# A depthwise 7x7 convolution recast: from 128-row banded filter weights to 28-row image weights in four quarters of the PE array

## The chip, the cores and the metric

The kernel runs on one core of one Trainium2 chip. The metric is device time in microseconds (us) of the whole program, from one launch. A core has five engines that run their own instruction streams: TensorE (PE in the profile, with its weight loads shown apart as PEld), VectorE (DVE), ScalarE (ACT), GpSimd (POOL) and SyncE (SP), which here only issues DMAs. All data are fp32.

## The reference

The input x is (32, 384, 28, 28): 32 images of 384 channels, 784 pixels each. Two layers follow each other. Cut to what matters:

```python
# layer 0: a ConvNeXt block
y = depthwise_conv7x7(x, dw_w, padding=3) + dw_b        # 384 channels, each with its own 7x7 filter
y = layernorm_over_channels(y) * ln_g + ln_b            # mean and variance over 384 channels per pixel
y = gelu(y @ w1 + b1)                                   # 384 -> 1536
gx = sqrt(sum_over_pixels(y * y)); nx = gx / (mean(gx) + eps)
y = grn_g * (y * nx) + grn_b + y
x = x + (y @ w2 + b2)                                   # 1536 -> 384
# layer 1: a gate
avg, mx, mn = mean, max, min of x over pixels           # per image and channel
logits = concat(avg @ W1.T, grouped(mx), mn @ W3.T) @ Wfc.T
out = sigmoid(logits[:, :, None, None] + x)
```

## The kernel before

**Two stages.** The first stage does the depthwise convolution of all 32 images and stores its result `yd` in device memory. It also prepares weights: the two matrices w1 and w2 are multiplied with fast (Strassen-like) schemes, so linear combinations of their blocks are formed once by GpSimd and ScalarE (`form_w`, stored to `u1d` and `u2d`), after w1 was centred for the layer norm (`center_w`). The second stage loops over images: `up` (products with `u1d`, PE line 979), gelu and norm, `down` (products with `u2d`, PE line 1139), `gate_store`. It starts with `finish`, which turns the sums over channels into the reciprocal standard deviation `rsd`. Its PE work is ordered image after image.

**The convolution on PE, before.** Partitions hold 4 image rows of 32 padded pixels (`PW` = 32). For each channel a banded 128x(128+2*96) matrix, `tmat`, holds the 7x7 filter in every position; it is loaded by one DMA for 8 channels from `fs`, a table of filter sequences in device memory, with an access pattern that shifts by one element per partition. `tmat` is the stationary operand (the weights), the turned image `xt` is the moving one. Per channel `conv` issues three products: the middle block (line 718, 224 moving columns, 7 row groups x 32 images), the rows that follow (line 720, 192 columns) and the rows before (line 722, 192 columns). Two channels share one PSUM tile `pc`.

**What feeds it and what follows it.** `load_x` brings a group of 4 images and 32 channels; `pad_x` copies it to a padded tile (ScalarE, line 506; at first also GpSimd); `turn_x` has PE transpose it, 7 pieces of 128x128 (line 516), and VectorE or ScalarE copy it out of PSUM into `xt` (lines 525 and 527). After the products VectorE transposes the PSUM tile in 32x32 blocks into `yt` (line 725) and adds it to `acc`, the sum over channels (line 729); ScalarE squares `yt` with the bias `dwb` added (line 735); GpSimd adds the squares to `ssum` (line 741). SP stores `yt` to `yd`. The last 16 channels are done in two halves of 16 images, so that the first image's result can be loaded back before the second half is done; `first_image` adds the bias on ScalarE while it copies image 0 to `room`.

**What sets the order.** Most instructions around the change are held in program order (`keep`); the rest (the forming of weight combinations, later the products) is placed by a list scheduler. SP's queue issues its DMAs in order. The layout of `yd` is by image row modulo 4 and reversed inside a row, so later readers use reversed, strided views (`rows`, and the quarter view in `down`).

Of the kernel before, what the change touches and what calls it, by code (L numbers as in the profile page):

```python
# [8 lines left out]
F32 = mybir.dt.float32  # L9
# [20 lines left out]
RW = 4  # L30
NJ = HW // RW
PW = P // RW
XC = 32
TC = 8
YC = 16
NB = P // XC
REACH = 3 * PW
MW = P + 2 * REACH
T0 = P - REACH

SN = 6 * PW + 7
S0 = T0 + REACH + P - 1 - 3 * PW - 3
FL = S0 + SN
YR = NJ * PW
SQ = 4
NQD = P // PW

# [166 lines left out]
def convnext_gate_kernel(  # L216
# [15 lines left out]
    N = NJ * B  # L232
# [6 lines left out]
    NY = C // YC  # L239
# [21 lines left out]
    stats = const.tile([P, SQ * YR + 2 * NJ * B], F32, name="stats")  # L261
    ssum = stats[:, : SQ * YR].rearrange("p (c n) -> p c n", n=YR)
    acc = stats[:, SQ * YR :].rearrange("p (c n) -> p c n", c=2)
# [34 lines left out]
    B0 = min(B, 16)  # L298

    def load_y(b):  # L300
        yi = yis[b] = yip.tile([P, CB, NQD, YR], F32, tag="yi", name=f"yi_{b}")

        with tc.issue_after(last_u2[-1]) if last_u2 else ExitStack():
            for cb in range(CB):
                ins = load_y_part(b, yi, cb, 0, P)
                if b == 1:
                    tc.keep_in_program_order(ins)
        load_rb(b)
# [24 lines left out]
    def rows(v):  # L333

        return v.rearrange("p q (j w) -> p (q j) w", w=PW)[:, :, ::-1][:, :, :HW]

    def normed(b, cbs=range(CB)):
# [5 lines left out]
        for cb in cbs:  # L343
            ins = nc.vector.scalar_tensor_tensor(  # L344
                accs[b][:, cb].rearrange("p (r w) -> p r w", w=HW), rows(yis[b][:, cb]),
                dwb_t[:, cb : cb + 1], rows(rbs[b]), ALU.add, ALU.mult,
# [43 lines left out]
    with ExitStack() as one:  # L390
        tp = one.enter_context(tc.tile_pool(name="tp", bufs=1))
        xtp = one.enter_context(tc.tile_pool(name="xtp", bufs=2))
        ufp = one.enter_context(tc.tile_pool(name="ufp", bufs=3))
        ycp = one.enter_context(tc.tile_pool(name="ycp", bufs=2))
        psx = one.enter_context(tc.tile_pool(name="psx", bufs=3, space=bass.MemoryType.PSUM))
        psb = one.enter_context(tc.tile_pool(name="psb", bufs=1, space=bass.MemoryType.PSUM))
        psc = one.enter_context(tc.tile_pool(name="psc", bufs=4, space=bass.MemoryType.PSUM))
        sqp = one.enter_context(tc.tile_pool(name="sqp", bufs=2))

# [18 lines left out]
        LENT = (3, 5, 7)  # L418
        AHEAD = B // NB
        NX = C // XC  # L420
        NG = B // NB
        NXI = 8
        xi_last = tp.tile([P, NT], F32, name="xi_last")
        GT = NX * NG
        xis = {}

        def load_x(i):

            k, g = divmod(i, NG)
            n = i % NXI  # L430
            t = xis[i] = xi_last if n == NXI - 1 else room[:, n * NT : (n + 1) * NT]
            base = x[g * NB, k * XC : k * XC + 1, :]
            nc.sync.dma_start(
                t,
                bass.AP(
                    tensor=base.tensor,
                    offset=base.offset,
                    ap=[[NT, XC], [C * NT, NB], [1, NT]],
                ),
            )  # L440

        dww = scratch([CB, 49])
        for i in range(AHEAD):
            load_x(i)
            if i == 1:
                nc.sync.dma_start(dww, dw_w.rearrange("(cb p) t -> p cb t", p=P))

        tab = ws[:, : CB * FL].rearrange("p (cb m) -> p cb m", m=FL)
        dwb = tp.tile([P, C], F32, name="dwb")
# [4 lines left out]
        grp_a = scratch([CB, R])  # L454


        NT2 = 4
        tmat = [tp.tile([P, TC, FL], F32, name=f"tmat_{i}") for i in range(NT2)]
        nc.vector.memset(tab, 0.0)

        def sequences(cb):
            nc.vector.tensor_copy(
                tab[:, cb, S0 : S0 + SN - 7].rearrange("p (y x) -> p y x", x=PW)[:, :, :7],
                dww[:, cb, :42].rearrange("p (y x) -> p y x", x=7),
            )
            nc.vector.tensor_copy(tab[:, cb, S0 + SN - 7 :], dww[:, cb, 42:])

        for cb in range(CB):
            sequences(cb)
            if cb == 0:  # L470
                nc.scalar.dma_start(fs[0][: 2 * TC, :], tab[: 2 * TC, 0, :])
                nc.scalar.dma_start(fs[0][2 * TC : P, :], tab[2 * TC :, 0, :])
        vrows = scratch([P], NV)
        zrow = scratch([FL], 1)
        nc.vector.memset(zrow, 0.0)
        NK = C // TC

        def load_t(s, parts=1):
            base = fs[s * TC // P]
            n = TC // parts  # L480
            for i in range(parts):
                nc.sync.dma_start(
                    tmat[s % NT2][:, i * n : (i + 1) * n, :].rearrange("p c m -> p (c m)"),
                    bass.AP(
                        tensor=base.tensor,
                        offset=base.offset + (s * TC % P + i * n) * FL,
                        ap=[[1, P], [1, n * FL]],
                    ),
                )


        NPAD = 3
# [881 lines left out]
```

## Time and profile before

| what | value |
|---|---|
| median of 3 runs | 3041.02 us (3037.3 to 3043.16) |
| the profiled execution | 3041.33 us, of which span 3039.6 us |
| PE busy over the span | 2996.2 us (99%) |
| PE's first convolution product starts | 17.69 us |
| PE's first product of `up` starts | 499.62 us |
| DMA in the first 500 us | 173.64 MB, 347 GB/s |

The span is what the profile covers; the 1.7 us around it are outside. A matmul's duration in a row is its latency; products overlap in the pipeline, so the time that one takes of PE is the step from its start to the next one's. An fp32 product appears as two weight loads and two matmuls.

### The profile page before, as it was taken

What the parts mean: (1) busy time and instruction counts of PE and PEld (TensorE: products, weight loads), DVE (VectorE), ACT (ScalarE), POOL (GpSimd) and SP (SyncE); (2) the same over time, 40 slices, a digit from 0 to 9 for tenths busy, and PEclk for the clock granted to TensorE, in tenths of its full rate; (3) what the DMA queues carried; (4) which work ended last, traced back from release to release, by engine and by line L of the source; (5) the groups of instructions that cost most, each with busy time, mean ns of one, the idle gap of its engine ahead of it and who ended that gap; (6) DMA issues with size and microseconds to landing.
All of it is one profiled execution on the core that took longest, in us unless ns stands there. A gap on an engine that the chain in (4) does not pass through costs nothing.

```text
span 3039.6 us, 43826 instructions
## 1 busy us (share of the span) xinstructions
PE 2996.2 (99%) x14436; PEld 2427.9 (80%) x14436; DVE 2036.2 (67%) x4643; ACT 1787.4 (59%) x2899; POOL 2431.9 (80%) x1811
## 2 busy tenths in 40 slices
PE   8999999899999999999999999999999999999998
PEld 8999997577777777777777777777777777777777
DVE  5767667776666666666666666666666666666665
ACT  4455554756666666666666666665666666666661
POOL 3367866688888888888888888888888888888897
PEclk9999999999999999999999999999999999999999
DMA  9899997546666666666666565566655666666645
GB/s 358 327 359 375 364 342 259 169 149 203 199 206 207 201 204 207 199 206 207 199 206 207 198 205 194 199 203 204 195 191 196 197 198 200 201 203 201 195 152 198
DMA packets 279256, 674.94 MB, mean 222 GB/s; under 512 B 24234, under 2 KB 99704, under 8 KB 273016
## 3 DMA queue, kind: packets, MB, share of 16 engines
q1 hardware_dynamic: 266472, 634.63, 61.9%
q10 hardware_dynamic: 12560, 37.51, 3.1%
q8 instruction: 117, 1.92, 0.2%
q14 instruction: 107, 0.88, 0.1%
HBM read 575.57 MB, written 96.48 MB: 221 GB/s over the span
## 4 chain that ended last, share of the span: by engine, by line
PE 91%; POOL 3%; DVE 3%; DMA 2%; issue 1%; ACT 1%; SPq 0%; ACTq 0%; DVEq 0%; POOLq 0%
PE ph_C L979 13%; PE ph_A L979 12%; PE ph_B L979 12%; PE pz_A L1139 8%; PE pz_C L1139 8%; PE pz_D L1139 7%; PE pz_F L1139 7%; PE pc L718 5%; PE pc L720 4%; PE pc L722 4%; PE pt L516 2%; PE pz_H L1139 2%; PE pz_I L1139 2%; POOL d_room L1102 2%; PE pz_E L1139 2%; DVE room L344 1%
## 5 line engine op out<-in xcount | busy, mean ns | idle before, releaser
L355 ACT ACTIVATE y<-y,vecs,gsc 128x784 f32<-128x784 f32 x375 | 359.9, 1030 | 467.0 <-DVE gsc L1047 467.0
L1102 POOL TENSOR_TENSOR d_room<-y 128x588 f32<-128x588 f32 x250 | 360.1, 1444 | 294.4 <-PE pz_B L1139 217.7
L927 ACT ACTIVATE y<-y,b1f 128x784 f32<-128x784 f32 x384 | 350.4, 945 | 196.7 <-DVE y L998 174.7
L979 PE MATMUL ph_C<-room,ws 128*128 128x392 f32 x1224 | 456.6, 494 | 4.1 <-DVE y L996 2.9
L1102 POOL TENSOR_TENSOR d_room<-d_room,y 128x588 f32<-128x588 f32 x308 | 442.8, 1442 | 16.7
L979 PE MATMUL ph_B<-room,ws 128*128 128x392 f32 x1220 | 451.7, 492 | 2.3 <-DMA ws<-u1d 2.3
L979 PE MATMUL ph_A<-room,ws 128*128 128x392 f32 x1220 | 453.0, 492 | 0.1
L979 PEld LDWEIGHTS ph_C<-room,ws 128*128 128x128 f32 x1224 | 230.6, 190 | 182.2 <-DVE y L996 21.7
L979 PEld LDWEIGHTS ph_A<-room,ws 128*128 128x128 f32 x1220 | 231.6, 190 | 170.5 <-POOL room L386 0.8
L979 PEld LDWEIGHTS ph_B<-room,ws 128*128 128x128 f32 x1220 | 231.0, 190 | 164.0 <-DMA ws<-u1d 2.9
L741 POOL TENSOR_TENSOR stats<-stats,sq 128x896 f32<-128x896 f32 x96 | 200.8, 2092 | 176.6 <-ACT sq L735 175.9
L947 ACT ACTIVATE stats<-y 128x784 f32<-128x784 f32 x381 | 326.7, 858 | 9.1
L1102 POOL TENSOR_TENSOR d_room<-y,d_room 128x588 f32<-128x588 f32 x214 | 306.5, 1438 | 27.0 <-PE pz_D L1139 15.9
L386 POOL TENSOR_TENSOR room<-room 128x392 f32<-128x392 f32 x298 | 298.9, 1019 | 11.6
L735 ACT ACTIVATE sq<-yt,dwb 128x224 f32<-128x224 f32 x368 | 157.2, 474 | 223.3 <-DVE yt L725 212.9
L1102 POOL TENSOR_TENSOR y<-y 128x588 f32<-128x588 f32 x180 | 258.3, 1435 | 6.5
L994 DVE TENSOR_TENSOR y<-y,ph_B 128x392 f32<-128x392 f32 x252 | 135.6, 558 | 157.9 <-ACT y L927 123.5
L992 DVE TENSOR_TENSOR y<-y,ph_C 128x392 f32<-128x392 f32 x386 | 213.4, 561 | 25.0 <-PE ph_C L979 0.3
L725 DVE STREAM_TRANSPOSE yt<-pc 128x448 f32<-128x448 f32 x184 | 119.3, 648 | 138.0 <-PE pc L722 99.5
L1139 PE MATMUL pz_A<-d_room,u 128*128 128x196 f32 x1050 | 204.4, 330 | 0.4 <-DMA u<-u2d 0.2
L718 PE MATMUL pc<-xt,tmat 128*128 128x224 f32 x736 | 200.8, 355 | 0.6 <-ACT xt L527 0.6
L1139 PEld LDWEIGHTS pz_A<-d_room,u 128*128 128x128 f32 x1050 | 178.4, 190 | 8.6 <-POOL d_room L1102 0.9
(299 smaller groups left out, 6410.8 us busy)
## 6 DMA issues: line engine op xcount, KB each, us to landing
u<-u2d SPq DMA_DIRECT2D x487, 384.0 KB, 3.7
ws<-u1d SPq DMA_DIRECT2D x380, 320.0 KB, 3.0
tmat<-fs SPq DMA_DIRECT2D x47, 1420.0 KB, 10.5
ws<-u2d SPq DMA_DIRECT2D x121, 384.0 KB, 3.8
yi<-yd SPq DMA_DIRECT2D x95, 448.0 KB, 6.4
yd<-yt SPq DMA_DIRECT2D x47, 896.0 KB, 7.0
x<-in_x SPq DMA_DIRECT2D x32, 1176.0 KB, 5.4
out<-x ACTq DMA_DIRECT2D x31, 1176.0 KB, 6.3
```

What stands on the lines that cost most here:

```text
L355: eng.activation(out, in_, AF.Identity, bias=add, scale=mul)
L386: tc.keep_in_program_order(eng.tensor_tensor(d, o[in0], o[in1], op))
L718: keep(nc.tensor.matmul(po, t[:, c, P : 2 * P], xc, start=True, stop=False))
L735: nc.scalar.activation(sq[:, cy % SQ + ci], yt[:, cy + ci], AF.Square, bias=dwb[:, cc + ci : cc + ci + 1], scale=1.0,)
L741: ins = nc.gpsimd.tensor_tensor(ssum, ssum, sq, ALU.add)
L927: ins = nc.scalar.activation(y, y, AF.Gelu, bias=b1f[:, f : f + 1], scale=1.0)
L947: ins = nc.scalar.activation(stats[:, :NT], ys[b][:, f, :], AF.Square, accum_out=ssqs[b][:, f : f + 1])
L979: ins = nc.tensor.matmul(banks[t, bk][:, :NH], wts[t, g][:, gi, :], o[opnd], start=(first == 1), stop=True, skip_group_check=True,)
L992: ins = nc.vector.tensor_tensor(d, d, p, ALU.add)
L994: ins = nc.vector.tensor_tensor(d, d, p, ALU.subtract)
L1102: eng.tensor_tensor(d[0], o[a][0], o[c][0], ALU.add if sign == "+" else ALU.subtract)
L1139: nc.tensor.matmul(pz[:, :NQ4], wt[:, i % UD, t, :], o[opnd][0][:, t, :], start=(first and t == 0), stop=(t == KD - 1), skip_group_check=True,
```

## The change

The roles in the convolution are swapped, and the array is used in four parts.

- **Layout.** A quarter of the partitions (32 of them, 28 used) holds one channel's 28 image columns. Four channels lie in four quarters. Free dimension: image rows x 32 images (`xts`), ordered so that 4 rows, 7 apart, x 32 images are 128 neighbouring columns.
- **Products.** The stationary operand is now x: 28 partitions x 128 columns (4 row quarters x 32 images). The moving operand is a 28 x (up to 196) band of the filter (`tmat`, now 128 x 446 for 8 channels), read backwards. For each of 13 relative input rows (`ROWS_IN`) one product gives all output rows that this input row reaches: 1 to 7 of 7 rows, 28 columns each. The four quarters' products follow each other in program order and write four PSUM banks. Per 8 channels that is 2 x 13 x 4 = 104 products; the products are `K` = 28 deep.
- **Feeding.** `load_x` brings 8 channels of all 32 images, partitions (quarter, image). `turn_x` is VectorE's 32x32 block transpose, two per 8 channels, 128x896 each, SBUF to SBUF. PE's transposes, `pad_x` and the copies out of PSUM go.
- **After the products** (`settle`). ScalarE copies each channel's result with its bias to `yt` (8 activations of 128x196; in the last step VectorE does four of them), VectorE adds four 128x392 pieces to `acc`, ScalarE squares 128x1568 at once, GpSimd adds 128x1568 to `ssum`. VectorE's transposes of PSUM tiles go.
- **The end of the stage.** The halving of the last 16 channels and `first_image` go. Image 0's last 16 channels go from `yt` to `room` by small DMAs inside SBUF (`direct`). `load_y(1)` is issued at the end of the stage, and `rb` of image 1 in `finish`.
- **Order of the rest.** w1 is loaded and centred earlier, and the combinations of w1 start at step 8 instead of 12, those of w2 at 19 instead of 24. Weight tiles `uf` have 6 buffers instead of 3, and are stored two steps after they were formed.
- **Second stage.** `yd` already holds the bias, and its layout is by plain quarters of the image. `normed` becomes one multiplication without the bias and without strided views; `stretch` and `down` lose their strided views. `finish` sums `ssum` over 8 pieces in three steps instead of 4 in two, and needs no transpose.

```diff
-RW = 4
-NJ = HW // RW
-PW = P // RW
-XC = 32
-TC = 8
...
+NQD = 4
+RQ = HW // NQD
+YR = RQ * HW
+PW = 32
+S0 = HW - 4
+FL = S0 + 6 * PW + 7
+TC = 2 * NQD
+NK = C // TC
+ROWS_IN = (3, 9, 2, -3, 4, 8, 1, -2, 5, 7, 0, -1, 6)
...
-            ins = nc.vector.scalar_tensor_tensor(
-                accs[b][:, cb].rearrange("p (r w) -> p r w", w=HW), rows(yis[b][:, cb]),
-                dwb_t[:, cb : cb + 1], rows(rbs[b]), ALU.add, ALU.mult,
+            ins = nc.vector.tensor_tensor(
+                accs[b][:, cb], flat(yis[b][:, cb]), flat(rbs[b]), ALU.mult
             )
...
-        psx = one.enter_context(tc.tile_pool(name="psx", bufs=3, space=bass.MemoryType.PSUM))
-        psb = one.enter_context(tc.tile_pool(name="psb", bufs=1, space=bass.MemoryType.PSUM))
-        psc = one.enter_context(tc.tile_pool(name="psc", bufs=4, space=bass.MemoryType.PSUM))
+        ufp = one.enter_context(tc.tile_pool(name="ufp", bufs=6))
+        ycp = one.enter_context(tc.tile_pool(name="ycp", bufs=4))
         sqp = one.enter_context(tc.tile_pool(name="sqp", bufs=2))
+        psc = one.enter_context(tc.tile_pool(name="psc", bufs=8, space=bass.MemoryType.PSUM))
...
+        def load_t(n):
+
+            cb, r = divmod(n * TC, P)
+            keep(
+                nc.sync.dma_start(
+                    tmat[n % NT2][:, : 2 * FL],
+                    bass.AP(
+                        tensor=fs[cb].tensor,
+                        offset=fs[cb].offset + r * FL,
+                        ap=[[2 * FL, NQD], [1, PW], [1, 2 * FL]],
+                    ),
+                )
+            )
...
+        def turn_x(n):
+
+            src = xis[n % NXI]
+            for g in range(2):
+                v = src[:, g * NT :]
                 keep(
-                    nc.tensor.transpose(
-                        pt[:, j - j0, :],
-                        xpad[i % NPAD][:, j * RW : (j + 1) * RW, :].rearrange("p r w -> p (r w)"),
-                        ident,
+                    nc.vector.transpose(
+                        xts[(2 * n + g) % NXT][:, 1:, :].rearrange(
+                            "p (k s) b -> p s k b", s=XK
+                        )[:, :NQD],
+                        bass.AP(
+                            tensor=v.tensor,
+                            offset=v.offset,
+                            ap=[v.ap[0], [YR, NQD], [HW, RQ], [1, PW]],
+                        ),
                     )
                 )
...
+        def conv(n, pcs):
+
+            t = tmat[n % NT2]
+            for g in range(2):
+                xt = xts[(2 * n + g) % NXT]
+                tv = t[:, g * FL : g * FL + 7 * PW].rearrange("p (y x) -> p y x", x=PW)
+                for a, i in enumerate(ROWS_IN):
+                    r0, r1 = max(0, i - 3), min(RQ, i + 4)
+                    s0 = 1 + XK * (i % RQ) + i // RQ
+                    for q in range(NQD):
+                        p0, p1 = PW * q, PW * q + HW
+                        keep(
+                            nc.tensor.matmul(
+                                pcs[q][:, g * YR + r0 * HW : g * YR + r1 * HW],
+                                xt[p0:p1, s0 : s0 + NQD, :].rearrange("p s b -> p (s b)"),
+                                tv[p0:p1, i - r1 + 4 : i - r0 + 4, :HW][:, ::-1, ::-1],
+                                start=(a == 0), stop=(a == len(ROWS_IN) - 1),
+                                skip_group_check=True,
+                            )
+                        )
+
+        def settle(n, pcs, yt):
+
+            last = n == NK - 1
+            for q in range(NQD):
+                for g in range(2):
+                    c = TC * n + 2 * q + g
+                    dst, src = yt[:, q, g, :], pcs[q][:, g * YR : (g + 1) * YR]
+                    if last and q >= 2:
+                        keep(nc.vector.tensor_scalar(dst, src, dwb[:, c : c + 1], None, ALU.add))
+                    else:
+                        keep(
+                            nc.scalar.activation(
+                                dst, src, AF.Identity, bias=dwb[:, c : c + 1], scale=1.0
+                            )
+                        )
+            for q in range(NQD):
+                keep(nc.vector.tensor_tensor(acc, acc, pcs[q][:, : 2 * YR], ALU.add))
+            sq = sqp.tile([P, TC * YR], F32, tag="sq", name=f"sq_{n}")
+            keep(nc.scalar.activation(sq, yt.rearrange("p q g n -> p (q g n)"), AF.Square))
+            keep(nc.gpsimd.tensor_tensor(ssum, ssum, sq, ALU.add))
...
+        for n in range(NK):
+            n_now = n
+            if 0 < n <= NK - NXI:
+                load_x(n + NXI - 1)
+            if n + 4 < NK:
+                load_t(n + 4)
...
+            pcs = [psc.tile([P, 512], F32, tag="pc", name=f"pc_{n}_{q}") for q in range(NQD)]
+            conv(n, pcs)
+            yt = ycp.tile([P, NQD, 2, YR], F32, tag="yc", name=f"yt_{n}")
+            settle(n, pcs, yt)
+            if n >= NK - 2:
+                direct(n, yt)
+            keep(nc.sync.dma_start(yd[:, TC * n : TC * (n + 1), :], yt.rearrange("p q g n -> p (q g) n")))
+            while stores and stores[0][0] + 2 <= n:
+                _, dst, u = stores.pop(0)
+                keep(nc.sync.dma_start(dst, u))
+            if n + 3 < NK:
+                turn_x(n + 3)
...
-            for n in (SQ // 2, 1):
-                to = ssum[:, :n] if n > 1 else s2.unsqueeze(1)
-                keep(nc.gpsimd.tensor_tensor(to, ssum[:, :n], ssum[:, n : 2 * n], ALU.add))
+            for n in (4 * YR, 2 * YR, YR):
+                keep(
+                    nc.gpsimd.tensor_tensor(
+                        ssum[:, :n], ssum[:, :n], ssum[:, n : 2 * n], ALU.add
+                    )
+                )
             forms_up(0, ("v", "x", "z"))
...
-                xh = xt[:, m, :].rearrange("p (j q w) -> p q j w", q=NQD, w=HW)[:, NQD - 1 - h]
-                pzh = pz[:, :NQ4].rearrange("p (j w) -> p j w", w=HW)
+                xh, pzh = xt[:, m, h * NQ4 : (h + 1) * NQ4], pz[:, :NQ4]
```

## The prediction

> **What bounds the kernel now.** I read the page's busy times first, then the windows of the first and second stage, then the groups of the first 500 us by form, then PE's timeline. The page's first lines, and its row of DMA over 40 slices of 76 us:
>
> ```profile
> PE 2996.2 (99%) x14436; PEld 2427.9 (80%) x14436; DVE 2036.2 (67%) x4643; ACT 1787.4 (59%) x2899; POOL 2431.9 (80%) x1811
> ...
> DMA  9899997546666666666666565566655666666645
> ```
>
> PE is the bound as a whole; DMA is close to full in the first six slices and never after. The windows (columns: window and its length, then busy us and count for PE, PEld, DVE, ACT, POOL, then PE clock, DMA share, GB/s):
>
> ```profile
> 0.00:25.00 25.00, 14.91 (x81) 12.85 (x82) 9.54 (x20) 10.52 (x18) 7.10 (x20) 0.97 0.84 295
> 25.00:500.00 475.00, 475.00 (x3095) 461.62 (x3094) 329.87 (x593) 238.69 (x493) 296.34 (x192) 1.00 0.93 350
> 500.00:650.00 150.00, 135.44 (x506) 91.32 (x505) 113.69 (x224) 86.91 (x145) 115.67 (x79) 0.98 0.56 187
> 650.00:3039.60 2389.60, 2370.82 (x10760) 1862.06 (x10758) 1583.08 (x3807) 1451.30 (x2245) 2012.83 (x1522) 1.00 0.60 198
> ```
>
> PE has no gap from 25 to 500 us: the convolution stage is PE's, at full clock. From 650 us on PE is 99.2% busy with products that the change leaves alone. So the change is worth what it does to the first 499.6 us, plus or minus something at the seam.
>
> PE's timeline shows what a product takes, by the step between starts (start, length, what, two passes each):
>
> ```profile
> 180.24 0.54 PE L718 MATMUL pc<-xt,tmat 128*128 128x224 f32 x2
> 180.62 0.49 PE L720 MATMUL pc<-xt,tmat 128*96 128x192 f32 x2
> 180.95 0.49 PE L722 MATMUL pc<-xt,tmat 128*128 128x192 f32 x2
> 181.27 0.54 PE L718 MATMUL pc<-xt,tmat 128*128 128x224 f32 x2
> ...
> 182.30 0.60 PE L516 MATMUL pt<-ident,xpad 128*128 128x128 f32 x4
> 182.74 0.54 PE L718 MATMUL pc<-xt,tmat 128*128 128x224 f32 x2
> ```
>
> A pass of 192 columns steps 0.33/2 = 0.163 us, so 0.84 ns a column and pass. One channel takes 181.27 - 180.24 = 1.03 us, and a transpose 0.44/4 = 0.11. The stage is 384 x 1.03 + 672 x 0.11 = 395 + 74 = 469 us, which is the window's 475. PE's weight loads, where the moving side is only 2 columns wide (line 614):
>
> ```profile
> 96.73 1.47 PEld L614 LDWEIGHTS pb<-lr,ws 128*128 128x128 f32 x12
> 98.03 0.40 PEld L516 LDWEIGHTS pt<-ident,xpad 128*128 128x128 f32 x3
> ```
>
> Twelve passes step (98.03 - 96.73)/12 = 0.108 us. That is the floor of a pass that loads 128 weight columns, however short its moving side.
>
> **The change on PE.** Removed: 469 us. Added: 48 steps x 104 products x 2 passes = 9984 passes. Their moving columns are 28 x (7, 1, 6, 1, 6, 2, 5, 2, 5, 3, 4, 3, 4), 1372 for each channel. With the floor of 0.108, a quarter's 13 passes take 0.164 + 2 x 0.141 + 2 x 0.118 + 8 x 0.108 = 1.546 us; two passes each, 3.09 us a channel. All then hangs on how many quarters work at once, which no row of the trace shows: every product there takes the whole array, or stands alone.
> - Four at once: 96 x 3.09 = 297 us.
> - Two at once: 594 us. None: 9984 x 0.108 = 1078 us.
>
> [...] an fp32 product is two passes (x2 above), and both passes of a quarter stand next to each other in the program. [...] 4992 x 105.5 columns x 0.84 ns = 443 us if the floor of 0.108 did not hold between passes. [...] I take the four quarters as independent (each with its own order)[...].
>
> Small PE work stays: 72 + 24 passes of weight centring at 0.11 and some transposes, 12 us.
>
> **What stands beside it.** Rows of the first 500 us by form (mean ns of one is after the busy time):
>
> ```profile
> L741 POOL TENSOR_TENSOR stats<-stats,sq 128x896 f32<-128x896 f32 x94 | 196.5, 2090 | 176.0 <-ACT sq L735 175.3
> L735 ACT ACTIVATE sq<-yt,dwb 128x224 f32<-128x224 f32 x368 | 157.2, 474 | 223.3 <-DVE yt L725 212.9 <-POOL u L594 3.8 <-POOL stats L741 3.7
> L725 DVE STREAM_TRANSPOSE yt<-pc 128x448 f32<-128x448 f32 x184 | 119.3, 648 | 138.0 <-PE pc L722 99.5 <-DMA yd<-yt 10.7 <-ACT xpad L506 8.1
> L525 DVE COPY xt<-pt 128x512 f32<-128x512 f32 x96 | 65.1, 679 | 9.0 <-PE pt L516 9.0
> L594 POOL TENSOR_TENSOR u<-u,ws 128x384 f32<-128x384 f32 x55 | 54.7, 1005 | 2.0
> L506 ACT ACTIVATE xpad<-room 128x784 f32<-128x784 f32 x79 | 66.5, 842 | 4.2 <-DMA room<-in_x 4.2
> ```
>
> Per step of 8 channels, where four quarters give PE 2 x 3.09 = 6.2 us:
> - POOL: an add over 1568. From 588 (1.44) and 896 (2.09) the slope is 2.1 ns, so 3.5 us; 48 of them 168 us in place of 200. The weight combinations stay: the rows of lines 588 and 594 sum to 98 us. Between steps 8 and 44 they add 2.7 a step, 6.2 in all: level with PE, and a little above it in steps 8 to 15, where the 27 us of their forms over 512 lie.
> - ACT: 8 activations of 196 with a bias. 784 takes 842 ns and 384 from PSUM 487, so 0.89 ns an element; a bias adds 92 (line 772, 934 ns for 784): 412 each, 3.3 us. The square over 1568: 1.54. Sum 4.9, 246 us with its share of combinations. Gone: 91 copies of 842 and 368 squares.
> - DVE: two transposes over 896. Between 648 (if the size cost nothing) and 1296 (all of it twice); the copies' slope of 1.05 ns gives 1.12, taken. Four adds over 392 at 0.56 (line 994). Sum 4.5, 215 us.
> - DMA: `tmat` falls from 70 to 48 x 0.228 = 11 MB, `yd` from 45 to 38.5; x stays 38.5, weights and combinations some 18. About 107 MB, at the 400 GB/s of the best slices 268 us, 5.6 a step, on SP's queue with its order of load, load, store; loads run four steps ahead, so a store that waits for `yt` delays nothing for a while.
>
> All fit under 6.2 but POOL, and each is within 30% of it. This cover is thin: if POOL is late, its square buffers (two) hold ACT, and ACT holds PSUM, and PE stops. I add 13 us for POOL's excess and 8 for filling at the start, 21 in all, between 0 and 80.
>
> **Start and seam.** The first product waits for filter table, store and load back as before (17.69 us): 18. VectorE's first transposes lie beside that wait. At the seam `up` begins with seven operands that don't need the last channels, 14 products x 0.66 = 9 us. Behind the last convolution product come ScalarE's copies (2), square (1.5), POOL's add (3.5) and then operands p, r, s (1.0 each), where before it was an add of 2.1; POOL's tree of adds is 3.5 us where it was 1.8. So x comes some 3 us later: +3 (between -8, since `load_y(1)` no longer stands between `rsd` and what waits for it on SP, and +8). In the second stage `normed` gets cheaper on DVE (line 344, 1197 ns); PE's 0.8% idle there leaves at most 5 us, and I take none.
>
> **Sum.** The stage ends at 18 + 297 + 12 + 21 = 348 instead of 499.6: -151.6. With +3: 3041.3 - 151.6 + 3 = 2893 for the profiled execution, which is 0.3 above the median of the runs. Predicted 2893; this case's own range is 2862 (no friction, a good seam) to 2950 (friction 80).
>
> **Rivals.**
> - *Quarters overlap in part.* [...] Short passes speak for it (8 of 13 are at the floor), and so does the number of instructions, 4 a product. 2950 to 3035; 443 us by array time alone gives 3024.
> - *Slower: program order holds between quarters.* Two at once: 18 + 594 + 12 = 624, all else hidden below it: 3041 + 124 + 3 = 3168. It decides once a step takes (499.6 - 18 - 12 - 3)/48 = 9.7 us, 47 ns a pass. For it: both passes of a quarter are neighbours, and line 614 shows the floor. [...]
> - *The quarters don't share at all* (weight loads one after another): 1078, ends at 1108, 3650. Nothing in the trace excludes it, since all its loads take the full array.
> - *POOL or DMA as the new bound* is inside my friction: POOL's 270 us, starting at 29, can't end before 299, and that is under 348.
>
> **How the numbers follow.** Chances: 0.59 for mine, 0.11 partial, 0.18 program order, 0.10 no sharing, 0.02 no change. A measurement of this kernel can tell about 0.2%, 6 us. Faster 0.70, same 0.02, slower 0.28. The range runs from 2860 to 3170: it takes in the partial case and most of the program-order case, and leaves out no sharing and the tails.
>
> **What would show it.** Right: the first product of `up` starts near 348 us; convolution passes step about 30 ns on average; two quarters' passes start within some ns of each other; POOL is over 85% busy between 80 and 330 us; DMA's share of the first 300 us stays above 0.8. Wrong: PE gapless with passes stepping 59 ns (program order) or 108 (no sharing); or gaps on PE that wait for `pc` (ScalarE, POOL) or for `xt` and `tmat` (DMA).

## The result: 6.2% slower

The changed kernel takes 3229.12 us (median of 4 runs, 3228.18 to 3232.37), the kernel before 3039.82 beside it. The ratio is 1.0624, with a 95% interval of 1.0606 to 1.0642. The forecast was 2893 us, and its range ended at 3170.

The profiled execution of the changed kernel took 3232.37 us, its span 3230.7. Its page, cut to the rows that answer those shown of before (busy times, then the clock and DMA over 40 slices of 81 us, then one group with busy us, mean ns and idle time before it):

```profile
PE 3119.1 (97%) x21348; PEld 2559.8 (79%) x21348; DVE 1912.1 (59%) x4350; ACT 1746.9 (54%) x2841; POOL 2399.1 (74%) x1774
...
PEclk9955555579999999999999999999999999999999
DMA  3335444445466666666666666566566666666645
...
L663 PE MATMUL pc<-tmat,xt 28*128 28x56 f32 (+6 forms) x9984 | 587.4, 430 | 67.6 <-DMA tmat<-fs 56.1
```

Two things were not there before. The granted clock is 0.5 over the convolution stage, where the old kernel had 1.00. And the DMA row, 8 or 9 in the first six slices before, is 3 to 5. The windows by stage (window and length, then busy us and count for PE, PEld, DVE, ACT, POOL, then clock, DMA share, GB/s):

```profile
0.00:25.00 25.00, 0.82 (x10) 0.85 (x14) 8.01 (x12) 1.49 (x2) 4.95 (x30) 1.00 0.30 105
...
164.00:692.00 528.00, 508.87 (x8533) 505.21 (x8534) 177.99 (x263) 181.60 (x395) 248.33 (x143) 0.50 0.45 168
692.00:850.00 158.00, 142.80 (x523) 95.36 (x522) 118.95 (x231) 87.76 (x142) 120.92 (x82) 0.96 0.52 165
850.00:3230.70 2380.70, 2363.37 (x10737) 1857.83 (x10735) 1573.07 (x3796) 1447.72 (x2240) 2003.87 (x1515) 1.00 0.61 196
```

From 164 to 692 us PE is 96% busy at half clock. From the first product of `up` on nearly all is as before: 2543.6 us, against 2540.0 in the old profile. One warning on the clock column: the trace records the clock only when it changes, and the first record lies at 153.6 us. Before it the profile fills in 1.00, though the passes there step as slowly as after 164 us. The timeline of PE shows both clocks (start, length, what, number of passes; neighbours of one line are drawn together):

```profile
24.18 24.84 PE L663 MATMUL pc<-tmat,xt 28*128 28x196 f32 x416 [24.18 <-DMA tmat<-fs]
...
153.75 6.51 PE L663 MATMUL pc<-tmat,xt 28*128 28x196 f32 x204
...
658.67 24.38 PE L663 MATMUL pc<-tmat,xt 28*128 28x196 f32 x412
687.11 2.95 PE L860 MATMUL ph_A<-ws 128*128 128x392 f32 x4 [4.07 <-DMA room<-yt]
```

At the start a pass takes 24.84/416 = 0.060 us on average, around 154 us 6.51/204 = 0.032, and near the end 24.38/412 = 0.059. A half step of 104 passes (13 products, 2 passes, 4 quarters) takes 3.25 us around 154 us and 6.12 at half clock. The first product of `up` starts at 687.11 us instead of 499.62, which is 187.5 of the 191.1 us that the span has grown.

What PE waited for (us in total, times, longest):

```profile
PE pc L663 <- DMA tmat<-fs: 56.1, 5, 26.2
PE pc L663 <- DVE stats L690: 10.7, 1, 10.7
PE pb L595 <- DMA ws<-in_w: 7.5, 1, 7.5
```

The groups of the other engines in the stage, by form:

```profile
L693 POOL TENSOR_TENSOR stats<-stats,sq 128x1568 f32<-128x1568 f32 x48 | 168.1, 3502 | 322.4 <-ACT sq L692 322.0
...
L685 ACT ACTIVATE yt<-pc,dwb 128x196 f32<-128x196 f32 x380 | 125.0, 439 | 447.9 <-PE pc L663 439.9 <-PE pf L543 8.0
L690 DVE TENSOR_TENSOR stats<-stats,pc 128x392 f32<-128x392 f32 x192 | 107.9, 562 | 370.0 <-ACT yt L685 351.9 <-DVE stats L690 1.0
L489 DVE STREAM_TRANSPOSE xt<-xi 128x896 f32<-128x896 f32 x72 | 75.5, 1087 | 10.0 <-DMA xi<-in_x 10.0
```

All three engines are busy for less than half of the stage and wait at the end of a chain that starts with PE. But for one wait of 10.7 us on VectorE, the stage is slow on PE and on its feeding alone.

### The profile page after: what moved, and what is told of

Read it like the earlier page. It is cut to its first block, busy times and chain, and to the rows that moved or that the text cites. A ratio compares the mean times of both kernels' runs of the same rounds, so it can differ in the third digit from the quotient of the medians.

```text
span 3230.7 us, 57070 instructions
## 1 busy us (share of the span) xinstructions
PE 3119.1 (97%) x21348; PEld 2559.8 (79%) x21348; DVE 1912.1 (59%) x4350; ACT 1746.9 (54%) x2841; POOL 2399.1 (74%) x1774
## 4 chain that ended last, share of the span: by engine, by line
PE 89%; DMA 5%; DVE 2%; POOL 1%; ACT 1%; SPq 1%; issue 1%; DVEq 0%; ACTq 0%; POOLq 0%
PE pc L663 15%; PE ph_C L860 13%; PE ph_A L860 12%; PE ph_B L860 11%; PE pz_A L1021 8%; PE pz_C L1021 8%; PE pz_D L1021 7%; PE pz_F L1021 7%; DMA tmat<-fs 2%; PE pz_H L1021 2%; PE pz_I L1021 2%; PE pz_E L1021 2%; DVE room L332 1%; PE pz_B L1021 1%; PE pz_G L1021 1%; POOL d_room L984 1%
## 5 line engine op out<-in xcount | busy, mean ns | idle before, releaser
L663 PE MATMUL pc<-tmat,xt 28*128 28x56 f32 (+6 forms) x9984 | 587.4, 430 | 67.6 <-DMA tmat<-fs 56.1
L663 PEld LDWEIGHTS pc<-tmat,xt 28*128 28x128 f32 x9984 | 583.7, 326 | 70.4 <-issue 33.1
L693 POOL TENSOR_TENSOR stats<-stats,sq 128x1568 f32<-128x1568 f32 x48 | 168.1, 3502 | 322.4 <-ACT sq L692 322.0
L685 ACT ACTIVATE yt<-pc,dwb 128x196 f32<-128x196 f32 x380 | 125.0, 439 | 447.9 <-PE pc L663 439.9
L690 DVE TENSOR_TENSOR stats<-stats,pc 128x392 f32<-128x392 f32 x192 | 107.9, 562 | 370.0 <-ACT yt L685 351.9
```

The costliest lines, as they stand in the source:

```text
L663: nc.tensor.matmul(pcs[q][:, g * YR + r0 * HW : g * YR + r1 * HW], xt[p0:p1, s0 : s0 + NQD, :].rearrange("p s b -> p (s b)"), tv[p0:p1, i ...
L685: nc.scalar.activation(dst, src, AF.Identity, bias=dwb[:, c : c + 1], scale=1.0)
L693: keep(nc.gpsimd.tensor_tensor(ssum, ssum, sq, ALU.add))
```

## The experiments

Three questions were open: why the clock is at half, what the waits for `tmat` are, and whether the four quarters really overlap. The last is answered by single records of the trace around 153.75 us: the first passes of quarters 0 to 3 start at 153.746, 153.753, 153.760 and 153.766 and last 428 ns each; the second passes of all four start behind them, at 154.016 to 154.036. So four passes were under way within 20 ns, where the old kernel's whole-array products stepped 0.33 to 0.38 us for two passes: the quarters run side by side.

All kernels below are the changed kernel with the edits shown; the edits are shortened (`keep`, tensors and offsets are left out). Times are one execution each unless a number of runs is given. The kernel before took 3039 to 3044 beside them.

### Loads that use more DMA engines (e1_split)

```diff
 def load_x(n, gs=(0, 2)):
-    base = x[:1, TC * n + g0, :]
-    dma_start(xis[n % NXI][:, g0 * NT : g1 * NT], ap=[[2 * NT, NQD], [C * NT, B], [1, (g1 - g0) * NT]])
+    for q in range(NQD):
+        base = x[:1, TC * n + 2 * q + g0, :]
+        dma_start(xis[n % NXI][q * B : (q + 1) * B, g0 * NT : g1 * NT], ap=[[C * NT, B], [1, (g1 - g0) * NT]])
 def load_t(n):
-    dma_start(tmat[n % NT2][:, : 2 * FL], ap=[[2 * FL, NQD], [1, PW], [1, 2 * FL]])
+    for q in range(NQD):
+        dma_start(tmat[n % NT2][q * PW : (q + 1) * PW, : 2 * FL], ap=[[1, PW], [1, 2 * FL]])
```

> The changed kernel, but the loads of x and of the filter bands are four DMAs each, one for every quarter of the partitions, so that the outer dimension of each access pattern is 32 and no longer 4. Theory 'few engines' (a DMA whose outer dimension is 4 is spread over 4 of the 16 DMA engines: the share was 0.26 and 107 GB/s while only such loads ran): the stalls of PE in the first 180 us (26 for the second filter band, 11 and 7 later, and 6 at the start) go, the granted clock stays 0.5, each half step of 104 passes stays 6.12 us, and the time is about 3229 - 50 = 3180. Rival 'slow memory' (32 images at a stride of 1.2 MB make the reads slow): the stalls stay, 3229.

Measured: 3174.59 us, 54.5 less than the changed kernel. The windows of this kernel:

```profile
0.00:25.00 25.00, 10.64 (x149) 9.98 (x152) 9.41 (x14) 1.49 (x2) 4.95 (x30) 1.00 0.73 185
123.40:632.00 508.60, 504.37 (x8518) 502.38 (x8512) 176.51 (x259) 180.46 (x393) 246.10 (x141) 0.50 0.59 171
```

In the first 25 us the DMA share goes from 0.30 to 0.73, and from 105 to 185 GB/s. The packets of the unsplit loads of x carry 6272 B and took 239 ns each in the median, about 26 GB/s for one engine; four engines give 105, and 105 was measured. A share of 0.30 is near 4 of 16 too (from 24 to 49 us, with these loads alone, it is 0.26 at 107 GB/s), and 4 is the outermost dimension of the access pattern. With the split, PE's idle time after its first product falls from 54.9 to 7.4 us and that first product starts at 13.3 instead of 24.2. The half steps still take 6.1 us (1707 passes in the 100 us from 200 us on) and the clock stays at 0.50. So the loads are one cause, worth some 55 us, and not the larger one.

### Products of the whole array among the others (e2_full, e3_both)

```diff
         for a, i in enumerate(ROWS_IN):
...
+            if a in (3, 7, 11):
+                matmul(pcs[0][:, 392:512], ones_f, ident[:, :120], start=True, stop=True)
```

e3_both has the split loads too.

> The changed kernel (with its DMAs as they were) plus three full-array products of 120 moving columns in each half step, written to unused columns of a PSUM bank; they compute nothing that is used. Theory 'clock' (four quarters do work at once, but products of 28 rows don't count as activity, so the array runs at half its clock): the granted clock goes to 1.0, a half step takes 3.25 + 0.65 to 4.2 us where no load is late, instead of 6.12. If 'few engines' holds too, the loads of a step take about 9.8 us on 4 engines, and the step is held at about 9.8: 48 x 9.8 = 470, time about 3080. Rival 'order' (program order lets two quarters overlap, 59 ns a pass at full clock) and rival 'issue' (59 ns a pass is what PE's sequencer takes for a weight load and a matmul): the half step gets longer by what is added, 6.12 + 0.65 = 6.8 or more, time about 3295.

> Both edits: four DMAs for each load, and three full-array products in each half step. Theory 'clock' with 'few engines': half step 4.0 to 4.2 us, stage about 18 + 48 x 8.3 + 12 + 20 = 448 us, time about 3041 - 50 = 2990, faster than before the change. Theory 'clock' with 'slow memory': no gain over the run with the full-array products alone, 3080. Rivals 'order' and 'issue': 3240 or more.

Measured: 3465.09 and 3441.33 us. Both forecasts missed. The timeline of e2_full shows what came instead:

```profile
301.79 0.78 PE L673 MATMUL pc<-ident,ones_f 128*128 128x120 f32 x2
302.50 2.71 PE L663 MATMUL pc<-tmat,xt 28*128 28x112 f32 x40
305.14 0.78 PE L673 MATMUL pc<-ident,ones_f 128*128 128x120 f32 x2
305.85 2.15 PE L663 MATMUL pc<-tmat,xt 28*128 28x168 f32 x32
307.93 0.78 PE L673 MATMUL pc<-ident,ones_f 128*128 128x120 f32 x2
308.64 2.06 PE L663 MATMUL pc<-tmat,xt 28*128 28x140 f32 x32
310.63 0.78 PE L673 MATMUL pc<-ident,ones_f 128*128 128x120 f32 x2
```

A half step takes 8.84 us (301.79 to 310.63) instead of 6.12, that is 0.91 us for each of the three whole-array products, where their two passes of 120 columns are 0.40 at half clock (2 x 120 x 0.84 ns x 2). From the start of a whole-array product to the next quarter product it is 0.71 us each time; what fills that time no row tells. The clock didn't rise in the stage: the passes keep stepping as at half clock (1248 to 1252 in 100 us from 200 to 500 us in e2_full, 1231 to 1252 in e3_both). The clock column says 1.00 there, as it does ahead of a first record. So three full products in a half step bought no clock here; by themselves these two runs say nothing for or against a cause of the half clock, only that this cure costs more than it brings.

### Rows or gaps: all 128 rows (e4_rows), and no gaps (e5_long)

```diff
# e4_rows
-for q in range(NQD):
-    p0, p1 = PW * q, PW * q + HW
+for q in range(NQD if a == 0 else 1):
+    p0, p1 = (PW * q, PW * q + HW) if q else (0, P)
# e5_long
-pcs[q][:, g * YR + r0 * HW : g * YR + r1 * HW]
+pcs[q][:, g * YR : (g + 1) * YR]
-tv[p0:p1, i - r1 + 4 : i - r0 + 4, :HW]
+tv[p0:p1, :RQ, :HW]
```

> Four DMAs for each load, and in place of the four quarters' products one product of 128 rows with the same columns, for 12 of the 13 input rows and the first quarter of the other (three quarter products stay there so that every PSUM bank is written). It leaves out three quarters of the convolution and sums over the quarters. The time pattern of a full clock is the same as that of four quarters at once, only the number of rows in one instruction differs. If the clock is withheld because of the rows ('clock: rows'): the granted clock is 1.0 and a half step takes about 3.09 + 0.3 = 3.4 us. If it is withheld because passes are short and weight loads leave gaps in the stream ('clock: gaps'): the clock stays 0.5 and a half step takes about 6.1 + 0.6 = 6.7. Rival 'order': with one instruction for four the passes can't overlap in any way, 3.4 at either cause; then the clock in the record has to be 1.0 here and in e2_full without a gain there. Rival 'issue': 32 passes of 59 ns, 1.9 us or what the array takes, 3.4.

> Four DMAs for each load, and every quarter product writes all 7 output rows (196 columns) for each of the 13 input rows, with the same filter rows each time; its convolution is not the reference's. Now no pass is shorter than its weight load, so the moving stream of each quarter has no gaps. Theory 'clock: rows' (a product of 28 rows isn't counted as activity, however dense): the clock stays at a half, a pass takes 196 x 1.67 = 0.327 us, a half step 26 x 0.327 = 8.5 us, the stage some 18 + 817 + 20, time about 3400. Theory 'clock: gaps': full clock, half step 4.26 to 4.5 us, time about 2990. A record without any clock change in the stage is to be read by the passes' steps, since the page fills it with 1.0.

Both have the split loads. Measured: 2987.8 and 3022.8 us. In e4_rows, which sums over the quarters and leaves out most of the products, the mean clock is 0.71 from 32 to 97 us and 1.00 from there to 441: 64 passes took 15.08 us at 80.47 us and 7.99 at 96.98. In e5_long, where every quarter product has 196 columns whatever it needs, the mean clock is 0.86 up to 84 us and 1.00 from there to 480. A window of e4_rows and one of e5_long:

```profile
97.00:441.00 344.00, 340.51 (x2775) 299.64 (x2774) 196.89 (x279) 190.96 (x415) 250.96 (x142) 1.00 0.88 259
84.00:480.30 396.30, 389.47 (x9139) 385.59 (x9131) 189.47 (x280) 192.65 (x419) 250.76 (x142) 1.00 0.78 229
```

So my theory of the moment, that the clock doesn't count quarter products because they use few rows, falls: with no gaps between them, 28-row products had a clock of 1.00 for 396 us. With a half step of 4.3 to 4.4 us (244 passes in 10.42 us at 199.78 us) they do 1.86 times the columns and are still 150 us faster than e1_split. I then took rows and time together, as an estimate from the steps above. Per half step a quarter has 2 x 1372 columns; at 2 x 0.84 ns that is 4.61 us of the 6.12, 75%. Times 28 of 32 rows it is 66%, and there the clock of e1_split stayed at 0.50. For e5_long it is 2 x 13 x 196 x 0.84 = 4.28 us of about 4.35, times 28/32, or 86%, and there it rose. Whether 32 rows at 75% are enough, two runs can't say; e9_k32 below tries it.

### A push to the clock (e6_burst, e7_each4, e8_each12)

```diff
+if n in (10, 20, 30):
+    for _ in range(40):
+        matmul(pcs[0][:, 392:512], ones_f, ident[:, :120], start=True, stop=True)
 conv(n, pcs)
```

This is e6_burst: 40 products of 128 rows and 120 columns. e7_each4 has 4 of them ahead of every step, e8_each12 has 12. All have the split loads.

> Four DMAs for each load, and before the products of steps 10, 20 and 30 a burst of 40 full-array products of 120 columns (unused results, in a PSUM bank before its own products start). Theory 'trap' (quarter products can hold the full clock but can't bring it back once it is lost, here to a stall at 121 us): after a burst the half steps stay at 3.2 to 3.5 us for 10 steps or up to the next stall, the stage ends near 430, time about 2970. Theory 'no credit' (they can't even hold it): the clock falls back within 3 to 10 us after each burst, half steps 6.12 again, time about 3190, a little above the run with the split loads alone (3174.6).

> Four DMAs for each load, and four full-array products of 120 columns ahead of each step's products, 8 passes, about as many as the weight centring has at steps 5 to 7, where the clock rose on the second occasion. If so much full-array work in 7 to 14 us is enough: clock mostly 1.0, a step 6.5 + 1.1 = 7.6 us, stage about 395, time about 2940. If it isn't: a step of 12.24 + 2 = 14.2, time about 3270.

> As the run with four full-array products ahead of each step, but with twelve (24 passes, 2.6 us at full clock, 5 at half). Enough to raise the clock in every step (a burst of 2 us did at 152 us): if the clock then holds to the next step, 6.5 + 2.8 = 9.3 us a step, stage about 480, time about 3020; if it falls within the step, between 9.3 and 17.5 a step, 3020 to 3410.

Measured: 3153.18, 3176.22 and 3081.94 us. The windows of e6_burst, after the first burst and before the second:

```profile
165.90:200.00 34.10, 32.10 (x838) 31.25 (x839) 14.87 (x21) 14.83 (x31) 20.09 (x11) 1.00 0.70 197
200.00:278.00 78.00, 78.00 (x1321) 77.80 (x1315) 25.88 (x37) 26.38 (x59) 45.52 (x27) 0.50 0.83 239
```

838 passes in 34.1 us against 1321 in 78. At half clock a 28-row pass steps 59 ns; behind the burst, from 173 to 183.2 us, 345 of them step 30. The clock is 1.00 from 165.9 to 200 us and from 281.9 to 322.9, around the first two bursts, and 0.50 in between. It fell at 200 us behind a pause of PE of 1.09 us, which ended at 199.51. So the 28-row products kept the full clock here for some 27 us behind the burst and did not get it back by themselves in 78 us, nor in e1_split from 123.4 to 632 us. Four full products a step lifted it for 68 and 65 us of the stage only (on the page of e7_each4 PEclk is 5 from 159 to 556 us). With twelve PEclk is 9 in every slice of the page of e8_each12, and the quarter products are busy for 334.5 us, against 514.3 in e7_each4. But the 1128 passes more (22476 against 21348) are paid for: 114 us, by an estimate of 120 columns x 0.84 ns for each.

### 32 rows (e9_k32), and with a push (e10_k32_each4)

The bands have room for 32 rows in each quarter. The four rows more are zero in `tmat`, so the sums are the same:

```diff
-p0, p1 = PW * q, PW * q + HW          # 28 rows
+p0, p1 = PW * q, PW * q + PW          # 32 rows
-nc.gpsimd.memset(t[:, 2 * FL :], 0.0)
+nc.gpsimd.memset(t, 0.0)              # and the split loads write 28 rows of each quarter
```

> Four DMAs for each load, and the quarter products take all 32 rows of a quarter instead of 28: the 4 rows more hold zeros in the moving filter bands (set once, the loads write 28 rows), so the convolution is the reference's and no pass gets longer. Theory 'activity is a mean over rows and time' (at half clock the changed kernel's quarters stream 75% of the time, 28/32 of it is 66%, which didn't raise the clock; a full-row pattern with about 76% and the dense quarter products with 87% did): now 75%, so the clock rises by itself, half steps are 3.2 to 3.4 us, the stage ends near 370, time about 2910. Theory 'gaps alone' (only the share of time in which a stream runs counts, rows don't): still 0.5, half steps 6.12, time 3175.

> 32 rows in each quarter and four full-array products ahead of each step. If 32 rows alone raise the clock: a step of 6.5 + 1.1, and time about 2955, worse than without them. If 32 rows come close to what is needed and don't reach it: the clock rises more often than in the run with 28 rows and four (where it was full for 68 and 65 us of the stage), time between 2955 and 3176. If rows don't count: 3176.

Measured: 3003.47 and 3015.01 us. e9_k32 differs from e1_split only in these rows, and is 171 us faster. Its page:

```profile
PEclk8898899999999999999999999999999999999999
DMA  8698866555666666666666666666666665566545
...
q8 instruction: 171, 2.80, 0.4%
```

The clock falls again and again, but now it rises again without a push: its mean is 0.75 from 25 to 100 us, 1.00 from 150 to 200, 0.81 from 200 to 250 and 0.90 to 0.97 in each 50 us from there to 500. Half steps take 3.2 us at full clock (126 passes in 4.07 to 4.12 us at 182.08 and 172.89 us). With the push PEclk is 8 in the first two slices of 75 us and 9 from there, and the quarter products are busy for 350.8 us instead of 365.8. But 376 passes more have to be paid for (38 us, by the same estimate), and the sum is no better: 3015 lies just above the 3003 to 3013 that the 32-row kernel takes in five executions (e14_k32_timed below).

### What is left (e11_lessx, e12_later, e14_k32_timed)

PE's waits in e9_k32:

```profile
PE pc L665 <- issue: 41.4, 38, 2.3
PE pc L665 <- DMA tmat<-fs: 14.5, 1, 14.5
PE pb L597 <- DMA ws<-in_w: 6.5, 1, 6.5
```

and its timeline from 165 us:

```profile
167.87 4.50 PE L665 MATMUL pc<-tmat,xt 32*128 32x196 f32 x127 [1.02 <-issue]
172.89 4.12 PE L665 MATMUL pc<-tmat,xt 32*128 32x28 f32 x126 [0.52 <-issue]
177.53 4.18 PE L665 MATMUL pc<-tmat,xt 32*128 32x140 f32 x128 [0.52 <-issue]
182.08 4.07 PE L665 MATMUL pc<-tmat,xt 32*128 32x84 f32 x126 [0.38 <-issue]
187.75 4.23 PE L665 MATMUL pc<-tmat,xt 32*128 32x84 f32 x126 [1.59 <-issue]
```

PE stops after every 126 to 128 passes, which is not a number of the computation (a half step has 104). A pass is two instructions. The page's queue q8, of kind "instruction", carried 171 packets and 2.80 MB, 16 KB each; over PE's 21348 passes that is 125 passes a packet. In e4_rows, with 14436 passes, it is 117 packets, 123 passes each, and in e8_each12, with 22476, it is 180, 125 each. So the stops come about as often as these packets. That PE waits there for the next packet, and that the 41 us are late packets, was my reading of these counts; no row of the trace shows what PE waits for. Short products put many instructions into little time: a half step is 208 of them in 3.2 us, 15 ns each.

e11_lessx and e12_later start from e9_k32.

```diff
# e11_lessx: of each pair of channels only the first 196 columns are loaded, x is zero elsewhere
-ap=[[C * NT, B], [1, (g1 - g0) * NT]]
+ap=[[C * NT, B], [1, (g1 - g0) * YR]]
# e12_later
-U1, U2, U2E = 8, 19, NK - 4
+U1, U2, U2E = 11, 22, NK - 4
-if n == 4:
+if n == 7:
-if 5 <= n < 8:
+if 8 <= n < 11:
-        center_w(FB + 4 * (n - 5) + i)
+        center_w(FB + 4 * (n - 8) + i)
```

e14_k32_timed is e9_k32 again.

> The 32-row kernel (loads split over the quarters, products of 32 rows) with a quarter of each x load: only the first 196 positions of each pair of channels are loaded, the other three quarters of the x tiles are zero, so that the convolution is of other data and the engines' work is the same. Of the 455 us that the stage takes with 32 rows, 41 us are short idle times of TensorE that the profile lays to nothing ('issue'), at a DMA share of 0.85 to 1.0. Theory 'instructions late': [...] the idle of the issue kind falls from 41 us to below 15, the stage ends at about 415 to 425 and the kernel at 2950 to 2975 us. Rival 'TensorE's own': the idle times stay, and the kernel takes 2995 to 3005 us.

> The 32-row kernel with the centring of w1 (forms at steps 8 to 10 instead of 5 to 7, the start at step 7 instead of 4, and the first u1 loads three steps later, the last u2 loads two steps apart from them). In the 32-row kernel TensorE waits 6.5 us for w1 at 57 us and then does the first 14.7 us of the centring at half clock. Theory: later, the centring finds w1 there and the clock full, so that it costs some 7.5 us instead of 14.7 and no wait: 10 to 20 us less than the 32-row kernel's 3003, that is 2983 to 2993 us. Rival: the loads that follow it then collide with x at the end of the stage, and the time stays at 3000 to 3005 us. Against the kernel before (3040) both are faster.

> The 32-row kernel once more, timed against the kernel before: it took 3003.5 in one look beside 3039.2, so 3000 to 3007 us and a ratio of 0.987 to 0.990 to the kernel before. If that look was a chance of where the stalls fell, since the clock's rises depend on them, the runs spread over some 30 us.

Measured for e11_lessx: 2980.01 us, `up` starting at 436.9 instead of 459.2 (although the first product starts 8.6 us later, behind the filling of the x tiles with zeros), and this first line of waits:

```profile
PE pc L665 <- issue: 27.0, 23, 3.4
```

That lies between the two forecasts: 23 stops where there were 38, at a DMA share of 0.50 and 0.71 from 100 to 150 and from 150 to 200 us, where it was 0.76 and 1.00. Fewer stops went with less x on the DMA engines, and e13_k32_only below, with a share of 0.29 to 0.52 in the first 500 us, has 4 of them, 2.3 us in all. Why 27 us are left with a quarter of x was not shown.

e12_later took 3005.33 us (4 runs, 2996.36 to 3013.22; ratio to the kernel before 0.9882, interval 0.9859 to 0.9904), e14_k32_timed 3011.58 (4 runs, 3006.78 to 3012.95; 0.9905, 0.9888 to 0.9921). The intervals overlap, so later centring isn't shown to bring anything, though its wait for w1 is gone from the trace. The full clock that the theory counted on isn't in its page either: PEclk is 8 in the first slice of 75 us and 7 in the second. With e9_k32's first execution at 3003.5 the 32-row kernel has a spread of some 10 us, more than the old kernel's 6. It is 1% faster than the kernel before and 7% faster than the changed one.

### 32 rows with the loads as they were (e13_k32_only)

```diff
-p0, p1 = PW * q, PW * q + HW
+p0, p1 = PW * q, PW * q + PW
```

> The changed kernel with 32 rows in each quarter product and nothing else: its loads are the changed kernel's own, one DMA for four quarters. (The four rows more hold filter values, not zeros, so that the sums take in terms that do not belong to them; the work is the same as with zeros.) Theory: the two causes add up nearly, the clock being worth about 170 us (3174.6 with split loads alone to 3003.5 with both) and the loads about 55 (3229 to 3174.6): 3050 to 3070 us, a clock that rises again after each stall, and half steps of 3.2 us between them. Rival: with loads that come late, the products never run densely enough for long, the clock stays at half in most of the stage although the rows are there, and the kernel takes 3150 to 3200 us.

Measured: 3193.94 us, in the range of the rival's forecast. Its clock and its waits:

```profile
PEclk7787777799999999999999999999999999999999
```

```profile
PE pc L663 <- DMA tmat<-fs: 127.8, 21, 32.5
PE pc L663 <- DVE stats L690: 49.6, 8, 14.6
```

With 32 rows the clock is up for a part of the time in every stretch of the stage: its mean is 0.60 to 0.91 in each 50 us from 50 to 500, at 0.50 in the changed kernel from 164 us on. PE stands still for 180 us after its first product, for 55 in the changed kernel. The two cures don't add up: loads alone bring 54.5 us, rows alone 35.2, both 225.6.

## Why the prediction was wrong

The sum of the prediction against the spans, all in us, PE's time laid to one of four terms up to the first product of `up`:

| term | predicted | changed kernel | e9_k32 |
|---|---|---|---|
| first product starts | 18 | 24.2 | 14.5 |
| quarter products | 297 | 587.1 | 365.4 |
| centring and the like | 12 | 20.9 | 18.7 |
| idle after the first product | 21 | 54.9 | 60.6 |
| `up` starts | 348 | 687.1 | 459.2 |
| rest, against 2540.0 before | +3 | +3.6 | +2.5 |

- **The step that failed is "Four at once: 96 x 3.09 = 297 us".** Four quarters at once, which no row of the old trace showed, was right: their passes start 7 ns apart, and a half step takes 3.25 us where the clock is full, 5% above the forecast. Its size was taken at the clock of the old stage, "at full clock", as if the clock belonged to the chip and not to the work. With the whole-array products of 192 and 224 columns the clock was 1.00 from 25 to 500 us; with 28-row products in their place it was 0.50 from 164 to 692, the half steps became 6.12 us, and the term 587. These 290 us are six sevenths of the miss of 339 in the stage. Shown: with products of the same count and 32 rows (e9_k32, 0.75 to 1.00), or of 28 rows without gaps (e5_long, 1.00 from 84 us on), the clock comes back.
- **What went with the clock.** PE's busy share did not: it is 504.37 of 508.60 us at a clock of 0.50 in e1_split, and 42.58 of 50 us at 1.00 in e9_k32 (150 to 200 us). Columns x rows did, in the four kernels for which I have the estimate: at half clock 66% in e1_split stayed at 0.50, while it rose with 75% in e9_k32 (with the same 6.12 us) and 86% in e5_long. At full clock 28-row products come to 2.31 of 3.25 us, times 28/32, or 62%, and kept it in e6_burst from 173 us up to the pause at 198.4. The falls stand behind pauses: 1.09 us in e6_burst, and in the changed kernel PE was busy for only 1.59 us of the 3.40 before 163.8, where the clock fell. The length of a pause alone doesn't tell: e9_k32 has pauses of up to 1.59 us from 150 to 200 us, with the clock at 1.00. What in the chip decides on the clock, and at which amount, no trace shows.
- **The floor of a pass.** 0.108 us for a weight load was right at full clock. At half clock it doubles too: 68 passes of 2 columns took 14.67 us at 110.17 us, 0.216 each, and a load is 327 ns long on average from 200 to 600 us, 184 from 154 to 160. Twice the forecast's 3.09 us is 6.18, and a half step took 6.12, of which the columns fill 75% by the estimate above. At full clock they fill still less of the time (2.31 of 3.25 us, 71%), so the full clock does not cure the gaps.
- **DMA.** "At the 400 GB/s of the best slices" took the rate from slices in which the DMA engines were all busy (a share of 1.01 at 410 GB/s from 80 to 100 us). The new loads had a share of 0.30 at the start, 105 GB/s, as 4 of 16 engines give. That is the start (+6) and most of the idle time (+34 against my friction, which was meant for POOL). My statement that loads run four steps ahead was true of the program and hid nothing, since the loads themselves were slow: PE waited 56.1 us for `tmat`.
- **Centring, +9.** 68 passes took 14.67 us at half clock; at 0.108 us each they would take 7.3.
- **Small slips** of the sum change nothing: with the seam's +3 the 3024 is 3028, and the lower end of 2862 is 2861.
- **POOL, ACT, DVE.** Predicted and measured for one instruction: 3.5 and 3502 ns, 412 and 439, 1.12 us and 1087 ns, 0.56 and 562. "This cover is thin" was never put to the test, as PE needed 12.2 us a step and not 6.2.
- **The seam** came out as forecast, +3.6 for +3, by luck in the main: 2.6 of it are `up`'s first eight passes at half clock (5.36 us up to 692.47 where the old kernel took 2.72), and the wait of 4.07 us for `room` just ahead of `up`, which was not forecast, stands in the table as idle time.
- **The rivals.** The time is near to the slower rival's 3168, and for another reason: in it quarter 1 would have started after quarter 0's first pass had ended, and the records show 7 ns between the starts of passes that last 428. The row that I had asked for as its mark, passes stepping 59 ns without gaps, is what the trace shows. A step of twice the length is no mark of half the overlap while the clock column is not read beside it. The rival of a partial overlap falls too: at full clock a half step is within 5% of four at once. What I should have costed is a clock that depends on the work: 0.50 with these products, 1.00 with the old ones.

## What to carry to other kernels

A duration read from a profile holds at the clock of that work (a half step took 3.25 us at full clock and 6.12 at half): before costing a change that makes TensorE's products shorter, shallower or more broken by waits, give the half clock its own case in the sum. In e6_burst the clock fell behind a pause of 1.09 us, and the 28-row products that had held it ran at half for the next 78 us. With products in parts of the array, try to fill the rows of their part, with zeros if need be; four idle rows of 32 decided 171 us here. Read the DMA share of a load beside the outermost dimension of its access pattern (here 0.26 to 0.30 with 4), and note that two cures may be worth little one by one and much together, so test them together before dropping either.

## What the runs showed of the hardware that was not expected

- Rows of zeros were worth time: with 32 rows instead of 28 and the same columns the clock rose again by itself (0.75 to 1.00 in the stretches of e9_k32, 0.50 from 123.4 to 632 us in e1_split), and the kernel was 171 us faster.
- PE's busy share did not go with the clock: 99% at 0.50 in e1_split (123.4 to 632 us), 85% at 1.00 in e9_k32 (150 to 200 us).
- A whole-array product among quarter products cost 0.91 us at half clock in e2_full, more than twice the 0.40 of its own passes.
- TensorE took 208 instructions in 3.2 us, and in e9_k32 it stopped behind every 126 to 128 passes in the rows from 168 to 192 us, 38 times in all, for up to 2.3 us; the packets of the page's queue of instructions come to 125 passes each. What it waits for the trace does not say.
- With one DMA of outermost dimension 4 a load, 105 GB/s moved in the first 25 us, at a share of 0.30; with four of outermost dimension 32, 185 at 0.73.
- The profile's clock is 1.00 until the first record. In e2_full it reads 1.00 from 100 to 800 us, though the passes of the stage step as at half clock (2.15 us for 32 of them at 305.85 us, 67 ns each).
